# The first feed-forward's input: from rows that are reloaded, scaled and transposed to columns that are stored once, reloaded and scaled

## The chip, the cores and the metric

The kernel runs on one core of one Trainium2 chip. The metric is the device time of one launch in microseconds (us); lower is better. A core has five engines that run side by side, each through its own list of instructions in order: TensorE (PE in the profile; its weight loads are shown as PEld), VectorE (DVE), ScalarE (ACT), GpSimd (POOL) and SyncE (SP), which here issues nearly all DMA transfers. They wait for one another through semaphores.

## The reference

A network of two gated layers over 4 sequences of 1024 tokens, 512 wide. Each layer normalizes its rows, runs an attention and a feed-forward network on the same normalized rows, and multiplies the two:

```python
x = L0_attn_x                                     # (4, 1024, 512)
xn = _layernorm(x, axis=-1)                       # eps 1e-5
s = _L0_attn_ref(xn, Wqkv, bqkv, Wout, bout, slopes)   # linear attention with decay, 16 heads
g = _silu(_L0_ffn_ref(xn, w_fc, w_proj))
x = x + s * g
xn = _layernorm(x, axis=-1)
s = _L1_attn_ref(xn, wq, wk, wv, wo)              # softmax attention, 16 heads
g = _silu(_L1_ffn_ref(xn, wq_gate, ...))
x = x + s * g
return x
```

Layer 0's feed-forward normalizes once more, with another epsilon, inside each of its two linear maps, and uses ternary weights:

```python
def bitlinear(x, w):
    xn = layer_norm(x)                            # eps 1e-6
    x_hat = absmax_quant(xn)                      # in value xn, but for rounding and a clip
    w_hat = ternarize_weights(w)                  # sign(round(w / (mean|w| + eps))) * mean|w|
    return einsum('bsd,od->bso', x_hat, w_hat)
h = gelu(bitlinear(xn, w_fc), approximate=False)  # 512 -> 2048
return bitlinear(h, w_proj)                       # 2048 -> 512
```

So the first feed-forward's input is a layer norm of a layer norm. Since the rows already have mean zero, the second norm is one factor for each token. That factor is what this case is about.

## The kernel before, in words

**Stages.** The 4096 tokens are 8 blocks (`NBLK`) of 512 tokens (`BLK`); a block is 4 tiles (`TPB`) of 128 rows, and the 512 columns are 4 groups of 128 (`KD`). The program runs four stages one after the other: layer 0's attention (up to about 630 us), layer 0's feed-forward (630 to about 1164), layer 1's attention, and layer 1's feed-forward. The change lies in the first two.

**Layer 0's attention.** The loop over `steps` runs over blocks and, in each, over four groups of heads. `moments0` and `norms0` compute four numbers for each token into `st0[blk]`: mean, 1/std, variance, and in column 3 the factor that takes a raw row minus its mean straight to the feed-forward's input. `turn0` normalizes a tile of rows on VectorE, transposes it on TensorE, and ScalarE copies it into `xnTs[blk]`, columns on partitions and tokens along the free axis, 1 MB a block. Beside this, `weights0` loads the feed-forward's weights piece by piece, two pieces a step: VectorE takes sums of their magnitudes and then makes them ternary. At the end, `first_rows` prepares the feed-forward's input for block 0, and the last block's output rows follow (`wo`, L333).

**Layer 0's feed-forward.** The loop over `g` takes one hidden step at a time: block `blk`, and `c`, the group of 128 out of 2048 hidden units. `hidden` multiplies the input by the ternary weights (fc, L588; 8 matmuls into one PSUM buffer of two), ScalarE applies gelu (h, L593), copies the result in a short format (hp, L598) and squares it (L600), VectorE makes the remainder of the split (hp, L601), and GpSimd and VectorE add h and its square to running sums (L609, L610). `proj` multiplies the hidden values into four accumulators, one for each tile of tokens, each two steps behind the one before (pj, L641). Every matmul input is split into two parts, hi and lo, in the short format, `xparts[blk]` for the block's input.

**What lies beside it.** While block `blk` is multiplied, the loop finishes block `blk - 1` and prepares block `blk + 1`. Finishing: `gate` at steps 1, 3, 5 and 7 for one tile of rows each (y on VectorE L658, tanh on ScalarE L660, two products on VectorE L661 and L662, an add on GpSimd L663, the store of the row tile by SP L664), `norm1` at step 12 and `turn_out` (xn on ScalarE L673, transposes tr_x L678). Preparing: at steps 0, 3, 6 and 9 SP loads a tile of the raw rows again (`x0f`, L705); at steps 2, 5, 8 and 11 `prep_in` has VectorE scale it (xq, L568); after the next step `turn_in` transposes it on TensorE (tr_xq, L576) and `split_in` splits it: hi on ScalarE (L230), lo on VectorE (L231), both reading PSUM.

**What sets the order.** TensorE's order is written out by hand, as the program has it. The order of the other engines is set by a planner that places instructions when it expects them to be ready; `keep_in_program_order` pins the ones it is given. Tiles come from pools with a fixed number of buffers (`bufs`), and an instruction waits until the buffer that it writes is free: fc has 2 PSUM buffers, so `fc` of step c+2 needs h of step c to have been read out; h has 3 and the loaded input tiles ("x") have 2.

Of the kernel before, what the change touches and what calls it, by code (L numbers as in the profile page):

```python
# [12 lines left out]
F32 = mybir.dt.float32  # L13
F32R = mybir.dt.float32r
# [5 lines left out]
P = 128  # L20
# [15 lines left out]
def kernel(ctx, tc, ins, out):  # L36
# [59 lines left out]
    nc.vector.memset(one_i, 1)  # L96

    xnT_d = [dram.tile([KD, P, N], F32, tag=f"xnT{b}", name=f"xnT_d{b}") for b in range(B)]

    def moments(pool, src, dst, name, pinned=False):  # L100

# [40 lines left out]
    def transpose_to(dst, src, name, on_scalar):  # L142

        t = tr(f"tr_{name}")
        for k in range(4):
            nc.tensor.transpose(t[:, k, :], src[:, k * P : (k + 1) * P], ident)
        if on_scalar:
            nc.scalar.copy(dst, t)  # L148
        else:
            nc.vector.tensor_copy(dst, t)  # L150
# [73 lines left out]
            w = nxt  # L224
            yield

    def split_in(xp, i, tp):

        hi, lo = [a[:, :, i * P : (i + 1) * P] for a in xp]
        nc.scalar.copy(hi.bitcast(F32R), tp)  # L230
        nc.vector.tensor_tensor(lo.bitcast(F32R), tp, hi, ALU.subtract)  # L231


    with ExitStack() as es:
# [52 lines left out]


        xnTs, vs, oTs = {}, {}, {}
        xparts = {}  # L290

        def moments0(blk):
            st = st0[blk]
            for i in range(TPB):
# [7 lines left out]
        def norms0(blk):  # L302

            st = st0[blk]
            nc.vector.tensor_tensor(st[:, :, 3], st[:, :, 1], st[:, :, 1], ALU.mult)
            nc.vector.tensor_tensor(st[:, :, 3], st[:, :, 3], st[:, :, 2], ALU.mult)
            inv_std(st[:, :, 3], eps6)
            nc.vector.tensor_tensor(st[:, :, 3], st[:, :, 3], st[:, :, 1], ALU.mult)

        def turn0(blk, i):  # L310
            st = st0[blk]
            t = blk * TPB + i
            xn = p2.tile([P, D], F32, tag="xn", name=f"xn0_{t}")
            nc.vector.tensor_scalar(
                xn, xt.pop(t), st[:, i, 0:1], st[:, i, 1:2], ALU.subtract, ALU.mult
            )
            transpose_to(xnTs[blk][:, :, i * P : (i + 1) * P], xn, f"x0_{t}", True)

        def values(blk, i):
            if i == 0:  # L320
# [123 lines left out]
            oTs[blk, g] = p2.tile([P, BLK], F32, tag="oT", name=f"oT0_{nm}", bufs=6)  # L444
            nc.scalar.copy(oTs[blk, g], o)

        def first_rows(i0):

            st = st0[0]
            for i in range(i0, i0 + 2):  # L450
                xq = p2.tile([P, D], F32, tag="xn", name=f"xq_{i}")
                nc.vector.tensor_scalar(
                    xq, xt.pop(i), st[:, i, 0:1], st[:, i, 3:4], ALU.subtract, ALU.mult
                )
                tp = tr(f"tr_xq_{i}")
                for k in range(KD):
                    nc.tensor.transpose(tp[:, k, :], xq[:, k * P : (k + 1) * P], ident)
                split_in(xparts[0], i, tp)

        es.enter_context(tc.manual_schedule(engines={mybir.EngineType.PE}))  # L460

        st = st0[0]
# [37 lines left out]
        for n, (blk, g) in enumerate(steps):  # L500

            if g < 2:
                jobs = [(output, blk - 1, 2 * g + c) for c in range(2)] if blk else []
            else:
                jobs = [(values, blk + 1, 2 * g - 4 + c) for c in range(2)] if blk + 1 < NBLK else []
            if n + 1 == len(steps):
                xparts[0] = xpair("xp_0")
                jobs = [(first_rows, 0), (first_rows, 2)]
            if g == 0 and blk + 1 < NBLK:
                moments0(blk + 1)  # L510
            pts = scores(blk, g, *cur[:2])
            for _ in range(2):
                next(beside, None)
            nxt = None
            if n + 1 < len(steps):
                nxt = project(*steps[n + 1])
            if jobs:
                jobs[0][0](*jobs[0][1:])
            outs(blk, g, cur[2], pts)
            if nxt:  # L520
                kd = turn_k(*steps[n + 1], nxt[1])
            if g < 2 and blk + 1 < NBLK:
                for i in range(2):
# [22 lines left out]
    with ExitStack() as es:  # L546
# [5 lines left out]
        def tr0(name):  # L552
            return pp.tile([P, KD, P], F32, tag="tr", name=name)

        hparts, sums, mvs, x1s, xnTp, x0fs = {}, {}, {}, {}, {}, {}
# [4 lines left out]
        def prep_in(blk, i):  # L560

            st = st0[blk]
            if i == 0:
                xparts[blk] = xpair(f"xp_{blk}")
            t = blk * TPB + i
            x = x0fs.pop(t)
            xq = p2.tile([P, D], F32, tag="xq", name=f"xq_{t}")
            nc.vector.tensor_scalar(  # L568
                xq, x, st[:, i, 0:1], st[:, i, 3:4], ALU.subtract, ALU.mult
            )  # L570
            return lambda: turn_in(blk, i, xq)

        def turn_in(blk, i, xq):
            tp = tr0(f"tr_xq_{blk}_{i}")
            for k in range(KD):
                nc.tensor.transpose(tp[:, k, :], xq[:, k * P : (k + 1) * P], ident)  # L576
            split_in(xparts[blk], i, tp)

        before = None

# [65 lines left out]
        def gate(blk, i):  # L646
# [7 lines left out]
            s = p2.tile([P, D], F32, tag="xq" if last else "s", name=f"s0_{t}")  # L654
            nc.sync.dma_start(out=s, in_=s0_t[t])
            sc = mv[:, 3, i : i + 1]
            y = p2.tile([P, D], F32, tag="y", name=f"y0_{t}")
# [27 lines left out]
                )  # L685

        es.enter_context(tc.manual_schedule(engines={mybir.EngineType.PE}))
        pending = None
        W = {}
        for g in range(NH0 * NBLK + 2 + 2 * TPB):  # L690
            blk, c = divmod(g, NH0)
# [7 lines left out]
                        )  # L699
                    )  # L700
            if blk < NBLK:
                if c % 3 == 0 and c < 3 * TPB and blk + 1 < NBLK:
                    t = (blk + 1) * TPB + c // 3
                    x0fs[t] = p2.tile([P, D], F32, tag="x", name=f"x0f_{t}")
                    nc.sync.dma_start(out=x0fs[t], in_=x_t[t])  # L705
                if c >= 2 and c % 3 == 2 and c < 2 + 3 * TPB and blk + 1 < NBLK:
                    pending = prep_in(blk + 1, (c - 2) // 3)
                hidden(blk, c)
                if blk == 0 and wpj0 + c < NH0:
                    ternary("pj", wpj0 + c, raw0("pj", wpj0 + c, "f"))  # L710
# [14 lines left out]
                gate(blk - 1, c // 2)  # L725
            if blk and c == 12:
                norm1(blk - 1, p2)
            if pending and c % 3 == 0:
                pending()
                pending = None  # L730
# [755 lines left out]
```

## Time and profile before

| | us |
|---|---|
| Median of 3 runs | 3150.0 |
| The three runs | 3148.52, 3150.00, 3150.66 |
| The profiled execution: its time | 3149.29 |
| The profiled execution: span from first to last instruction | 3147.5 |
| TensorE busy in the span | 3088.4 |
| VectorE busy | 1905.1 |
| GpSimd busy | 1501.4 |
| ScalarE busy | 1196.1 |
| Mean granted TensorE clock | 0.994 of full speed |

Most of GpSimd's time is layer 1's attention (844.8 us in one group of additions there), so the sum over the program says little of the stage that is changed. In the time line a row is: start, duration, engine, line, operation, output<-inputs by name, sizes, the number of neighbours taken together, and in brackets the engine's idle time before it and what ended that. Times are microseconds from the span's start.

### The profile page before, as it was taken

Reading aid. Unit: us, or ns where it says so; the run is one execution under the profiler, and the core shown is the slowest. Engines: PE = TensorE matmul, PEld = TensorE weight load, DVE = VectorE, ACT = ScalarE, POOL = GpSimd, SP = SyncE. Lnnn points to the kernel's source line nnn. Section 1 sums busy time; section 2 is a strip of 40 time slices with the busy share of each in tenths; the row PEclk is TensorE's granted clock in tenths of the full one; section 3 lists DMA queues with packets and bytes.
Section 4 is the critical chain, followed back from the end, with each engine's and each line's share of the span. In section 5 each row is a group of like instructions: output and inputs, shape, how many; then the busy total and the mean of one; then the engine's idle time right before and its main releaser. Section 6 shows DMA issues by size and latency. Waiting matters only on the chain.

```text
span 3147.5 us, 61092 instructions
## 1 busy us (share of the span) xinstructions
PE 3088.4 (98%) x26233; PEld 1765.4 (56%) x26233; DVE 1905.1 (61%) x2638; ACT 1196.1 (38%) x1696; POOL 1501.4 (48%) x615
## 2 busy tenths in 40 slices
PE   9999999999999998999999999999999999999998
PEld 5555555578777874443344444334444435888887
DVE  4444555468888775656656555555555684566655
ACT  3111111155555542444444444444444444333332
POOL 0000000034444344898888988888888970000001
PEclk9999999999999999999999999999999999999999
DMA  3111111122222231100001000010000013322211
GB/s 131 54 54 54 54 57 44 38 64 91 81 81 71 94 138 38 48 9 8 8 17 40 12 12 15 20 35 14 10 17 15 12 44 100 119 75 66 67 51 55
DMA packets 97799, 158.46 MB, mean 50 GB/s; under 512 B 13040, under 2 KB 26864, under 8 KB 97392
## 3 DMA queue, kind: packets, MB, share of 16 engines
q1 hardware_dynamic: 96704, 151.33, 15.5%
q8 instruction: 207, 3.39, 0.5%
q0 software_dynamic: 816, 3.15, 0.3%
q14 instruction: 72, 0.59, 0.1%
HBM read 104.10 MB, written 41.94 MB: 46 GB/s over the span
## 4 chain that ended last, share of the span: by engine, by line
PE 84%; DVE 11%; issue 2%; ACT 2%; POOL 1%; SPq 1%; DMA 0%; ACTq 0%; POOLq 0%; DVEq 0%
PE sk L1027 9%; PE sq L1000 8%; PE y L1046 8%; PE qk L350 7%; PE gate L1218 5%; PE up L1218 5%; PE dn L1240 5%; PE v1ps L856 4%; PE v0ps L324 3%; PE wo L333 3%; PE wo L856 3%; PE wq L856 3%; PE fc L588 3%; PE wk L856 3%; PE pj L641 3%; PE sk L1033 2%
## 5 line engine op out<-in xcount | busy, mean ns | idle before, releaser
L1067 POOL TENSOR_TENSOR part<-part,pT 128x2048 f32<-128x2048 f32 x184 | 844.8, 4591 | 25.7 <-ACT pT L1038 16.5
L1004 DVE TENSOR_REDUCE mx<-sq 128x2 f32<-128x1024 f32 x512 | 603.3, 1218 | 384.3 <-PE sq L1000 383.1
L1038 ACT ACTIVATE pT<-sk 128x1024 f32<-128x1024 f32 x512 | 496.3, 1021 | 619.4 <-PE sk L1033 616.1
L1027 PE MATMUL sk<-wqT,wkT 32*128 32x512 f32 x2048 | 332.5, 645 | 4.3 <-DVE mx L1004 4.3
L1000 PE MATMUL sq<-wkT,wqT 32*128 32x512 f32 x2048 | 322.5, 641 | 6.1 <-ACT pT L1038 5.1
L1046 PE MATMUL y<-pT,v 128*32 128x512 f32 x2048 | 276.3, 610 | 0.2 <-ACT pT L1038 0.2
L609 POOL TENSOR_TENSOR sums<-sums,h 128x512 f32<-128x512 f32 x112 | 162.9, 1455 | 228.9 <-ACT h L593 223.8
L641 PE MATMUL pj<-wpj,hp 128*128 128x512 f32 x1024 | 265.2, 397 | 5.8 <-DVE hp L601 4.9
L588 PE MATMUL fc<-xp,wfc 128*128 128x512 f32 x1024 | 261.1, 397 | 2.9 <-ACT h L593 2.0
L1262 POOL TENSOR_TENSOR th<-th,x 128x512 f32<-128x512 f32 x31 | 40.1, 1295 | 457.9 <-DVE th L1261 377.0
L1033 PE MATMUL sk<-mT,onesr 2*128 2x512 f32 x1024 | 239.3, 788 | 2.2 <-DVE mT L1016 2.2
L357 POOL TENSOR_TENSOR qd<-qT,wqkv 128x512 f32<-128x512 f32 x32 | 41.1, 1285 | 405.0 <-ACT qT L355 379.1
L350 PE MATMUL qk<-xnT,wqkv 128*128 128x512 f32 x512 | 230.0, 602 | 0.7 <-ACT xnT L148 0.7
L641 PEld LDWEIGHTS pj<-wpj,hp 128*128 128x128 f32 x1024 | 190.0, 188 | 58.2 <-DVE hp L601 17.4
L588 PEld LDWEIGHTS fc<-xp,wfc 128*128 128x128 f32 x1024 | 187.3, 188 | 44.4 <-ACT h L593 5.0
L1027 PEld LDWEIGHTS sk<-wqT,wkT 32*128 32x128 f32 x2048 | 99.9, 184 | 138.0 <-issue 111.4
L1218 PE MATMUL gate<-xp,wf 128*128 128x512 f32 x704 | 174.1, 389 | 0.0
L1065 POOL TENSOR_TENSOR part<-pT,pT 128x2048 f32<-128x2048 f32 x31 | 141.2, 4555 | 69.0 <-ACT pT L1038 68.8
L1218 PE MATMUL up<-xp,wf 128*128 128x512 f32 x704 | 173.8, 389 | 0.0
L1240 PE MATMUL dn<-wf,hp 128*128 128x512 f32 x704 | 173.5, 389 | 0.0
L601 DVE TENSOR_TENSOR hp<-h,hp 128x512 fp32r<-128x512 f32 x128 | 116.9, 913 | 76.2 <-ACT hp L598 76.1
L350 PEld LDWEIGHTS qk<-xnT,wqkv 128*128 128x128 f32 x512 | 95.2, 191 | 112.8 <-issue 104.2
(219 smaller groups left out, 4543.4 us busy)
## 6 DMA issues: line engine op xcount, KB each, us to landing
s<-s SPq DMA_DIRECT2D x96, 256.0 KB
x<-x SPq DMA_DIRECT2D x36, 256.0 KB
x<-in_x SPq DMA_DIRECT2D x32, 256.0 KB
raw_fc<-in_w_fcT SPq DMA_DIRECT2D x32, 256.0 KB
x0f<-in_x SPq DMA_DIRECT2D x32, 256.0 KB
x0r<-in_x SPq DMA_DIRECT2D x32, 256.0 KB
x<-th SPq DMA_DIRECT2D x32, 256.0 KB
xnT<-xnT_d SPq DMA_DIRECT2D x8, 1024.0 KB
```

The lines of the kernel that those rows point to most:

```text
L350: nc.tensor.matmul(a, lhsT=wqkv[k][:, c0 : c0 + P], rhs=xnTs[blk][:, k, :], start=(k == 0), stop=(k == KD - 1),)
L588: nc.tensor.matmul(a, lhsT=wfc[k][:, c * P : (c + 1) * P], rhs=xp[n][:, k, :].bitcast(F32R), start=(k == 0 and n == 0), stop=(k == KD - 1 ...
L641: nc.tensor.matmul(ds[i], lhsT=hparts[blk, c][n][:, i * P : (i + 1) * P], rhs=wpj[c], start=(c == 0 and n == 0), stop=(c == NH0 - 1 and n ...
L856: nc.tensor.matmul(out[r0 : r0 + HD, :], lhsT=lhsT[:, r0 : r0 + HD], rhs=rhs, start=start, stop=stop,)
L1000: nc.tensor.matmul(sq[:, hh, :], lhsT=qT[r, q0 : q0 + P], rhs=kT[r, n * 512 : (n + 1) * 512], start=True, stop=True,)
L1004: nc.vector.tensor_reduce(mx[:, qt, 2 * pair : 2 * pair + 2, n], sq, AX.X, ALU.max)
L1027: nc.tensor.matmul(sks[h // 2][:, h % 2, :], lhsT=kT[r, kb * P : (kb + 1) * P], rhs=qT[r, qh * 512 : (qh + 1) * 512], start=True, stop=False,)
L1038: nc.scalar.activation(pT[:, 2 * pair : 2 * pair + 2, :], sks[pair], AF.Exp, scale=QKS)
L1046: nc.tensor.matmul(y[r, :], lhsT=v[:, kb, r], rhs=pT[:, h, :], start=(kb == 0), stop=(kb == TB - 1),)
L1067: add.tensor_tensor(parts[u], parts[u], pT, ALU.add)
L1218: nc.tensor.matmul(a, lhsT=ws[n, c][:, k, :], rhs=xp[m][:, k, :], start=(k == 0 and m == 0), stop=(k == KD - 1 and m == 1),)
L1240: nc.tensor.matmul(ds[i], lhsT=hparts[blk, c][n][:, i * P : (i + 1) * P], rhs=w, start=(c == 0 and n == 0), stop=(c == NH1 - 1 and n == 1),)
```

## The change

The normalized, transposed rows that the attention has anyway (`xnTs[blk]`) are stored to DRAM, 1 MB a block, as soon as a block's four tiles are turned. `norms0` leaves out its last multiply, so that column 3 of the statistics is the factor from the normalized row to the feed-forward's input, and this is stored to DRAM too, as a row of 512 numbers. The feed-forward then loads column groups of the transposed rows (256 KB each) where it loaded row tiles, and once a block the row of factors, broadcast to all 128 partitions (256 KB). GpSimd multiplies a column group by the factors, ScalarE makes hi, and GpSimd makes lo. The loads are issued at steps 0, 3, 6 and 9 and the split at steps 2, 5, 8 and 11, as before. `prep_in`, `turn_in`, `split_in` and `first_rows` go. Block 0's input is loaded two steps before the end of the attention and split in its last step, where `output` of the last attention block follows directly. The row load of `x0r` in `gate` stays.

```diff
+    xn0T_d = [
+        dram.tile([KD, P, BLK], F32, tag=f"xn0T{i}", name=f"xn0T_d{i}") for i in range(NBLK)
+    ]
+    more_d = dram.tile([NBLK, BLK], F32, tag="more", name="more_d")
...
-    def split_in(xp, i, tp):
-
-        hi, lo = [a[:, :, i * P : (i + 1) * P] for a in xp]
-        nc.scalar.copy(hi.bitcast(F32R), tp)
-        nc.vector.tensor_tensor(lo.bitcast(F32R), tp, hi, ALU.subtract)
+    def ffn_in(blk, k, tile):
+
+        if k == 0:
+            xparts[blk] = xpair(f"xp_{blk}")
+            mores[blk] = tile("more", f"more_{blk}")
+            nc.sync.dma_start(out=mores[blk], in_=more_d[blk].partition_broadcast(P))
+        x = tile("x", f"x0f_{blk}_{k}")
+        tc.keep_in_program_order(nc.sync.dma_start(out=x, in_=xn0T_d[blk][k]))
+
+        def split():
+            hi, lo = [a[:, k, :] for a in xparts[blk]]
+            nc.gpsimd.tensor_tensor(x, x, mores[blk], ALU.mult)
+            nc.scalar.copy(hi.bitcast(F32R), x)
+            nc.gpsimd.tensor_tensor(lo.bitcast(F32R), x, hi, ALU.subtract)
+
+        return split
...
             inv_std(st[:, :, 3], eps6)
-            nc.vector.tensor_tensor(st[:, :, 3], st[:, :, 3], st[:, :, 1], ALU.mult)
+            nc.sync.dma_start(out=more_d[blk].rearrange("(i p) -> p i", p=P), in_=st[:, :, 3])
...
             transpose_to(xnTs[blk][:, :, i * P : (i + 1) * P], xn, f"x0_{t}", True)
+            if i == TPB - 1:
+                nc.sync.dma_start(out=xn0T_d[blk].rearrange("k p n -> p k n"), in_=xnTs[blk])
...
-        def first_rows(i0):
-
-            st = st0[0]
-            for i in range(i0, i0 + 2):
-                xq = p2.tile([P, D], F32, tag="xn", name=f"xq_{i}")
-                nc.vector.tensor_scalar(
-                    xq, xt.pop(i), st[:, i, 0:1], st[:, i, 3:4], ALU.subtract, ALU.mult
-                )
-                tp = tr(f"tr_xq_{i}")
-                for k in range(KD):
-                    nc.tensor.transpose(tp[:, k, :], xq[:, k * P : (k + 1) * P], ident)
-                split_in(xparts[0], i, tp)
...
-            if n + 1 == len(steps):
-                xparts[0] = xpair("xp_0")
-                jobs = [(first_rows, 0), (first_rows, 2)]
...
             if n + 2 == len(steps):
 
-                for i in range(TPB):
-                    xt[i] = p2.tile([P, D], F32, tag="x", name=f"x0f_{i}", bufs=4)
-                    tc.keep_in_program_order(nc.sync.dma_start(out=xt[i], in_=x_t[i]))
+                first_in = [
+                    ffn_in(
+                        0, k,
+                        lambda tag, name: p2.tile(
+                            [P, BLK], F32, tag={"more": "xn"}.get(tag, tag), name=name,
+                            bufs={"x": 4}.get(tag, 2),
+                        ),
+                    )
+                    for k in range(KD)
+                ]
+            if n + 1 == len(steps):
+                for split in first_in:
+                    split()
...
             if blk < NBLK:
-                if c % 3 == 0 and c < 3 * TPB and blk + 1 < NBLK:
-                    t = (blk + 1) * TPB + c // 3
-                    x0fs[t] = p2.tile([P, D], F32, tag="x", name=f"x0f_{t}")
-                    nc.sync.dma_start(out=x0fs[t], in_=x_t[t])
-                if c >= 2 and c % 3 == 2 and c < 2 + 3 * TPB and blk + 1 < NBLK:
-                    pending = prep_in(blk + 1, (c - 2) // 3)
+                if blk + 1 < NBLK:
+                    if c % 3 == 2 and c < 3 * KD:
+                        split()
+                    if c % 3 == 0 and c < 3 * KD:
+                        split = ffn_in(
+                            blk + 1, c // 3,
+                            lambda tag, name: p2.tile([P, BLK], F32, tag=tag, name=name),
+                        )
                 hidden(blk, c)
...
-            if pending and c % 3 == 0:
-                pending()
-                pending = None
```

More of the change, by code (lines that the diff above doesn't have):

```diff
@@ L225, in weights0 @@
             yield
-    def split_in(xp, i, tp):
-        hi, lo = [a[:, :, i * P : (i + 1) * P] for a in xp]
-        nc.scalar.copy(hi.bitcast(F32R), tp)
-        nc.vector.tensor_tensor(lo.bitcast(F32R), tp, hi, ALU.subtract)
+    def ffn_in(blk, k, tile):
[11 more added lines that the diff above has]
+        return split
+    xparts, mores = {}, {}
     with ExitStack() as es:
@@ L289 @@
         xnTs, vs, oTs = {}, {}, {}
-        xparts = {}
         def moments0(blk):
@@ L553, in tr0 @@
             return pp.tile([P, KD, P], F32, tag="tr", name=name)
-        hparts, sums, mvs, x1s, xnTp, x0fs = {}, {}, {}, {}, {}, {}
+        hparts, sums, mvs, x1s, xnTp = {}, {}, {}, {}, {}
         for c in range(wpj0, NH0):
@@ L558 @@
         rows = p2.tile([P, D], F32, tag="rows", name="rows", bufs=1)
[L560 to L577, printed above, removed]
         before = None
@@ L653, in gate @@
             nc.sync.dma_start(out=x, in_=x_t[t])
-            s = p2.tile([P, D], F32, tag="xq" if last else "s", name=f"s0_{t}")
+            s = p2.tile([P, D], F32, tag="more" if last else "s", name=f"s0_{t}")
             nc.sync.dma_start(out=s, in_=s0_t[t])
@@ L727 @@
                 norm1(blk - 1, p2)
-            if pending and c % 3 == 0:
-                pending()
-                pending = None
             if 0 < blk < NBLK and c >= 14:
```

## The prediction

> **What bounds the kernel now.** I read the page's busy times first, then two stretches of the stage that the change touches (one steady block, 831 to 898 us), then the time line in it.
>
> ```profile
> PE 3088.4 (98%) x26233; PEld 1765.4 (56%) x26233; DVE 1905.1 (61%) x2638; ACT 1196.1 (38%) x1696; POOL 1501.4 (48%) x615
> ```
> ```profile
> 831.00:866.00 35.00, 34.42 (x158) 27.39 (x158) 31.07 (x54) 17.45 (x30) 15.03 (x10) 1.00 0.36 113
> 866.00:898.00 32.00, 31.62 (x153) 25.64 (x152) 23.97 (x39) 20.94 (x35) 13.49 (x9) 1.00 0.15 43
> ```
> The columns of the second fence are stretch, length, then busy PE, PEld, DVE, ACT, POOL. TensorE is 98% busy here too, so work taken off it looks like pure gain. But in the first half of a block, where gating runs, VectorE is 31.07 of 35.00 busy. The time line shows why that matters:
>
> ```profile
> 854.97 1.81 DVE L662 SCALAR_TENSOR_TENSOR th<-th,mv,s 128x512 f32<-128x512 f32 x1
> 856.70 0.68 DVE L601 TENSOR_TENSOR hp<-h,hp 128x512 fp32r<-128x512 f32 x1
> 856.86 1.67 POOL L663 TENSOR_TENSOR th<-th,x0r 128x512 f32<-128x512 f32 x1 [0.63 <-DVE th L662]
> 857.31 1.77 DVE L610 TENSOR_TENSOR sums<-sums,sq 128x512 f32<-128x512 f32 x1
> 859.61 0.67 DVE L231 TENSOR_TENSOR xp<-tr_xq,xp 128x512 fp32r<-128x512 f32 x1
> ...
> 861.92 0.74 DVE L658 SCALAR_TENSOR_TENSOR y<-rows,mv,pj 128x512 f32<-128x512 f32 x1
> 862.69 0.72 ACT L660 ACTIVATE th<-y,mv 128x512 f32<-128x512 f32 x1 [4.47 <-DVE y L658]
> 863.32 0.67 ACT L593 ACTIVATE h<-fc,gam_fc 128x512 f32<-128x512 f32 x1
> 864.04 2.11 PE L588 MATMUL fc<-xp,wfc 128*128 128x512 f32 x8 [0.26 <-ACT h L593]
> ```
> Two things. First, a VectorE operation with two SBUF inputs takes 0.68 alone and 1.77 to 1.81 while GpSimd works; the subtract of the input split (L231), which has one input in PSUM, takes 0.67 in the same stretch. Second, the last four lines are a chain: y on VectorE, its tanh on ScalarE, the gelu h queued behind that, and fc_10, which needs the PSUM buffer h gives back. TensorE waits only 0.26, but without slack: whatever makes y later moves fc_10.
>
> **The change part by part.** *TensorE.* Each block loses 4 groups of transposes:
>
> ```profile
> 809.51 0.60 PE L576 MATMUL tr_xq<-ident,xq 128*128 128x128 f32 x4
> 809.86 2.09 PE L588 MATMUL fc<-xp,wfc 128*128 128x512 f32 x8
> 811.78 2.00 PE L641 MATMUL pj<-wpj,hp 128*128 128x512 f32 x8
> 813.63 1.99 PE L588 MATMUL fc<-xp,wfc 128*128 128x512 f32 x8
> 815.45 2.02 PE L641 MATMUL pj<-wpj,hp 128*128 128x512 f32 x8
> 817.31 0.60 PE L678 MATMUL tr_x<-ident,xn 128*128 128x128 f32 x4
> ```
> The step with a group is 809.51 to 813.63 = 4.12, the next 813.63 to 817.31 = 3.68: a group is worth 0.44 in the pipeline (not its 0.60). 32 groups make 14.1 us, the most that TensorE can gain directly.
>
> *The other engines, per block.* VectorE loses 4 xq (0.73 mean) and 4 subtracts (0.67). ScalarE's 4 casts stay, now from SBUF (0.62 like L598's, not 0.57). GpSimd gets 8 operations of 128x512: a multiply by the token scale and a subtract for each of 4 column tiles, with the cast between them. Nearest rows: L357's multiply 1.285 alone, L609's add 1.455 as a mean of alone and contended. 8 × 1.3 = 10.4 more on an engine 28.5 of 67 busy: room as an engine. The cost is VectorE's.
>
> Here the row is that th (L662) and sums (L610) go from 0.7 to 1.8 beside GpSimd. The Trainium skill, "SBUF — State Buffer", section "Who interferes with whom", says that a VectorE operation with two SBUF inputs and a GpSimd operation exclude each other for the length of the instruction, whoever is first, and that one with at most one SBUF input is free. It speaks against this change: the removed subtract (PSUM input) took no part, all eight new operations do. By the rule, each holds the other for its full lone time (1.30 and 0.68). The trace's alternating pairs are shorter: three GpSimd adds from 867.69 take 5.16 with a VectorE operation between them, so one pair is about 1.71, of which I give 1.16 to GpSimd and 0.55 to VectorE (VectorE's contended operations end about 0.55 after GpSimd's). I take the trace's holds and keep the rule's for the range. Demand for the shared port per block by lone times: before, 19 GpSimd × 1.3 + 39 VectorE × 0.6 + 1.8 for xq = 50 of 66.6 us (829.69 to 896.31, from one block's sums to the next's on TensorE); after, 27 × 1.3 + 23.4 = 59 of the 64.8 that four groups less would leave.
>
> I then walked one block with the new order of each engine (numbers behind a name are steps or tiles; the multiply, cast and subtract of column tile k are mult_k, hi_k, lo_k): GpSimd runs sums_6, the add of row tile 10, sums_7, mult_2, lo_2, sums_8; ScalarE runs hi_2, then the tanh of tile 11, then h_8. GpSimd holds 1.16, VectorE 0.55. On before's time axis:
> - fc_8 starts about 854.5, as h_6 ends 854.45; nothing is gained over 854.89 but 0.4, though TensorE would be ready at 853.99.
> - GpSimd: sums_6 to 855.6, then, between VectorE's th, hp_6 and sums_6, tile 10's add 856.7 to 857.9, sums_7 to 859.6. The row tile's store goes out at 857.95; the load of column tile 2 stands behind it on SP's queue, 858.3, and is there 2.8 later (first load of the program: 0.75 issue to 3.52 use; x0f 630.78 to 633.65), 861.1. So mult_2 waits for it: it ends 862.3, cast hi_2 862.9. Tanh of tile 11 is queued behind that cast on ScalarE: 863.55; h_8 864.2; fc_10 starts 864.25 against 864.04 before, while TensorE was ready about 862.
> - lo_2, sums_8 and tile 11's add share the port; tile 3's load is issued 868.5, lands 871.3; mult_3 ends 872.5, hi_3 873.1, h_10 (behind it) 873.75, so fc_12 starts 873.8 against 872.02: 1.8 late. At step 12 the missing transposes give some back: 877.5 against 876.47.
> - VectorE, in turn, is held 1.16 by each of GpSimd's further operations and is behind when gating ends: sums_12 ends 882.8, the norm's small operations (2.6) 885.4, xn 886.2. The transposes tr_x of the finished rows, which stand in TensorE's order, start 886.2 against 883.92.
>
> So a steady block is 2.3 longer (1.4 if the loads land in 2.2; 4.0 with the rule's full holds). Sum:
> - blocks 2 to 6, which run beside the next block's preparation: 5 × 2.3 = 11.5
> - block 1 the same plus 1.7, because cast hi_1 is also in front of hp_5 on ScalarE: 4.0
> - block 0, where VectorE also quantizes the last weights and 16 GpSimd operations meet 25 of VectorE in eight steps (hp_2 about 646 against 640.69, partly absorbed): 5, between 3 and 8
> - end of the attention stage: the transpose groups at 609.28 and 614.79 and a wait of 0.68 at the second go, so the first output product starts about 614.1 and not 615.71: −1.6
>
> Total +18.9. The profiled execution took 3149.3 (span 3147.5 and 1.8 around it): 3168. The median of the runs is 0.7 above it, which I leave out.
>
> *Costed at nothing, with the cover.* Eight 1 MB stores and the 256 KB broadcast loads: DMA share is 0.16 to 0.17 from 100 to 595 us, and 0.36 at most in the block above. The first store meets the weight loads at 2 to 26 us (share 0.93); it can push the decay table by about 3 us, to 25, so dec is ready about 33.5; the first product needs it at 40.3. The scale's store waits on SP for VectorE's reciprocal and holds back the ternary weights' loads behind it (107.6 to 109.6), whose reductions stand on VectorE: their buffer is needed at 114.8 and they would end about 112.9; uncovered it is up to 1 us in each of 7 blocks. Its four-byte elements are 512 a block; no row prices them, nobody waits before the next stage. Zero to 7 in all for these; I take zero, since the margin exceeds 0.6 everywhere that I followed it. ScalarE's casts, 0.05 longer: ScalarE is idle 17 of 35.
>
> **The rivals.**
> - *Heavier lock (20%).* The full lone durations hold. 5 × 4.0 + 5.7 + 8 − 1.6 = +32: 3181. For: the rule, and L610 at 1.77. Against: the shorter pairs at 867.69.
> - *Gain just eaten (17%).* Loads or GpSimd are a little earlier than I walk, tanh and h come as before, and TensorE starts the same steps at the same time with a wait in place of the transposes: about 3148. For: that chain holds to within 0.3 in before already. Against: nothing takes the 1.8 of fc_12 away.
> - *The other side: GpSimd's work hides (18%).* All 14.1 comes, with 1.9 of waits for xq and 0.7 at the stage's start: 16.7, so 3133. The place is h_8: it must end before TensorE is ready for fc_10, about 862, so mult_2 must be done by about 860.3. My walk has 862.3. It would take a load that doesn't wait for the store of the tile before, or ScalarE running tanh ahead of the cast. For: VectorE has 5.6 less to do per block; GpSimd is under half busy.
> - *The change does nothing of what it says*: the transposes are named by line and gone, so I give this no share.
>
> **How the numbers follow.** My own case: 45%, 3156 to 3176, at 3168. 0.2% is 6.3 us, about what a measurement of this kernel tells from no change. Faster (under 3143): 0.18, GpSimd's work hidden. Same: 0.17. Slower: 0.45 + 0.20 = 0.65. The range goes from 3141 (into the gap between no change and the gain, with the fast case out) to 3190 (heavy lock plus the uncovered stores); it leaves out 0.18 below and little above.
>
> **What would show it.** In after: tr_xq gone; GpSimd busy up by 80 to 100 us, its multiplies idle before with a DMA (x0f) as releaser; hp (L601) and sums (L610) means up from 913 and 1082 ns; fc idle behind h of ScalarE up from 2.0 us to over 15, or tr_x waiting for xn; a steady block 69 instead of 66.6. I am wrong if fc's waits stay under 5 us and hp's mean doesn't rise (then the gain comes), or if the attention stage grows by more than 2 us (then the stores were not covered).

## The result and the profile after

The changed kernel took 3258.31 us (median of 5 runs, 3251.15 to 3267.73) against 3150.66 (5 runs, 3148.52 to 3153.63): 1.0343 times the time of before, interval 1.0331 to 1.0356. It is slower, as forecast, but by 108 us and not by 19, and far outside the range.

Where do the 108 us lie? The table takes from both time lines the start of the first fc, of each group that sums a block's statistics (ms), and of layer 1's first product (wk):

| stretch | before | after | difference | forecast |
|---|---|---|---|---|
| start to first fc (attention stage) | 630.49 | 711.47 | +80.98 | −1.6 |
| first fc to block 0's sums | 67.31 | 69.89 | +2.58 | +5 |
| block 1 | 65.31 | 68.87 | +3.56 | +4.0 |
| blocks 2 to 6, each (mean) | 66.57 | 70.73 | +4.17, five times 20.84 | +2.3, five times 11.5 |
| last block and the end of the stage | 68.16 | 68.14 | −0.02 | 0 |

Three quarters of the loss are in a stage where a small gain was expected. The engines' totals of after show little of it, only that TensorE's share fell from 98% to 95%:

```profile
PE 3102.6 (95%) x26105; PEld 1766.3 (54%) x26105; DVE 1886.8 (58%) x2566; ACT 1194.5 (37%) x1696; POOL 1595.9 (49%) x679
```

GpSimd has 94 us more, as forecast. TensorE has 128 instructions fewer and is busy 14 us longer, so its instructions themselves became slower. The time line of after from 125 us on shows where the stage's time goes (rows as before; SPq and the line number mark a DMA issue by SP):

```profile
125.11 0.38 SPq L324 DMA_DIRECT2D more_d<-st  x1
125.54 0.97 SPq L183 DMA_DIRECT2D raw_fc<-in_w_fcT  x2
...
138.60 0.69 DVE L188 TENSOR_REDUCE part_fc<-raw_fc 128x1 f32<-128x512 f32 x1 [13.51 <-DMA raw_fc<-in_w_fcT]
...
139.80 0.68 DVE L387 TENSOR_TENSOR kd<-k0t,kdec 128x512 f32<-128x512 f32 x1
...
140.53 1.11 PE L151 MATMUL tr_x<-ident,xn 128*128 128x128 f32 x4 [10.47 <-DVE kd L387]
...
141.44 5.02 PE L351 MATMUL wo<-wout,oT 128*128 128x512 f32 x8
```

The same place in before:

```profile
114.31 0.66 PE L146 MATMUL tr_x<-ident,xn 128*128 128x128 f32 x4 [0.35 <-DVE kd L369]
114.80 3.60 PE L333 MATMUL wo<-wout,oT 128*128 128x512 f32 x8
```

The token factors go out at 125.11. The weight load issued 0.43 later is there only 13 us after its issue. VectorE's reduction stands waiting for it with kd behind it, and TensorE waits 10.47 for kd. VectorE's waits of this stage say that it happened seven times (columns: total, times, longest):

```profile
DVE part_fc L188 <- DMA raw_fc<-in_w_fcT: 23.9, 2, 13.5
DVE part_pj L188 <- DMA raw_pj<-in_w_projT: 22.8, 2, 11.5
DVE neg_fc L213 <- DMA raw_fc<-in_w_fcT: 22.5, 2, 13.8
...
DVE neg_pj L213 <- DMA raw_pj<-in_w_projT: 13.0, 1, 13.0
```

Together 82.2 us. The stretches from 126 to 144 show the second part of the price (the column before the last two is the granted clock, as a share of full speed):

```profile
126.00:128.00 2.00, 2.00 (x15) 1.29 (x16) 0.00 (x0) 0.00 (x0) 0.78 (x1) 1.00 0.64 145
...
134.00:136.00 2.00, 0.00 (x0) 0.00 (x0) 0.00 (x0) 0.00 (x0) 0.00 (x0) 0.51 0.19 5
...
142.00:144.00 2.00, 2.00 (x3) 0.68 (x2) 0.24 (x1) 0.27 (x1) 0.00 (x0) 0.50 0.69 182
```

After about 4 us without work the clock is halved and stays so for a while after work returns: the eight wo matmuls at 141.44 take 5.02 instead of 3.60. Over the stage the groups of after, and then wo of before, read

```profile
L351 PE MATMUL wo<-wout,oT 128*128 128x512 f32 x256 | 124.1, 633 | 0.0
...
L151 PE MATMUL tr_x<-ident,xn 128*128 128x128 f32 x128 | 22.9, 307 | 61.0 <-DVE kd L387 59.0 <-DVE st L479 1.2 <-DVE xn L330 0.5
...
L333 PE MATMUL wo<-wout,oT 128*128 128x512 f32 x256 | 114.6, 592 | 0.0
```

The transposes tr_x took 20.0 before, with 4.9 of waiting for kd. TensorE's waits in this stage grew by 64.6 us (tr_x for kd 54.1, qk 6.9, u 3.6); most of the other 16 us is the half clock, 9.5 of it in wo alone.

The second place is the one that the prediction walked. This is after's step 8 to 10 of a steady block, 91.45 us later than in before:

```profile
950.55 0.42 SPq L239 DMA_DIRECT2D x0f<-xn0T_d  x1
...
953.36 1.29 POOL L243 TENSOR_TENSOR x0f<-x0f,more 128x512 f32<-128x512 f32 x1 [1.51 <-DMA x0f<-xn0T_d]
954.68 0.62 ACT L244 CAST xp<-x0f 128x512 fp32r<-128x512 f32 x1 [5.32 <-POOL x0f L243]
955.20 0.72 ACT L653 ACTIVATE th<-y,mv 128x512 f32<-128x512 f32 x1
...
955.83 0.67 ACT L586 ACTIVATE h<-fc,gam_fc 128x512 f32<-128x512 f32 x1
...
956.55 3.68 PE L581 MATMUL fc<-xp,wfc 128*128 128x512 f32 x8 [1.93 <-ACT h L586]
```

Load, multiply, cast, tanh, h, fc_10: the forecast's chain link by link. The y of that tile was there at 953.66, so the tanh stood behind the cast. TensorE's wait for h before fc_10 grew from 0.26 to 1.93.

The eight matmuls of this fc_10 take 3.68 instead of 2.11, because the clock is halved here too:

```profile
957.00:959.00 2.00, 2.00 (x6) 1.55 (x5) 1.96 (x3) 1.97 (x5) 1.37 (x2) 0.50 0.00 0
```

It happens three times in after's feed-forward, for about 3.5 us each, and not in before's. It does not explain the longer blocks: those that have it in blocks 2 to 6 took 70.36 and 70.37, the others 70.80 to 71.23.

### The profile page after: what moved, and what is told of

Same layout as the page of the kernel before. It is cut to its first block, busy times and chain, and to the rows that moved or that the text cites. A ratio compares the mean times of both kernels' runs of the same rounds, so it can differ in the third digit from the quotient of the medians.

```text
span 3256.5 us, 60856 instructions
## 1 busy us (share of the span) xinstructions
PE 3102.6 (95%) x26105; PEld 1766.3 (54%) x26105; DVE 1886.8 (58%) x2566; ACT 1194.5 (37%) x1696; POOL 1595.9 (49%) x679
## 4 chain that ended last, share of the span: by engine, by line
PE 76%; DVE 9%; DMA 5%; ACT 4%; issue 3%; POOL 3%; SPq 1%; POOLq 0%; ACTq 0%; DVEq 0%
PE sk L1018 9%; PE sq L991 8%; PE y L1037 8%; PE qk L368 5%; PE gate L1209 5%; PE up L1209 5%; PE dn L1231 5%; PE v1ps L847 3%; PE wo L847 3%; PE wq L847 3%; PE wk L847 3%; PE wo L351 3%; PE v0ps L342 3%; PE fc L581 2%; PE sk L1024 2%
## 5 line engine op out<-in xcount | busy, mean ns | idle before, releaser
L581 PE MATMUL fc<-xp,wfc 128*128 128x512 f32 x1024 | 262.8, 400 | 25.0 <-ACT h L586 24.3
L602 POOL TENSOR_TENSOR sums<-sums,h 128x512 f32<-128x512 f32 x112 | 171.0, 1527 | 137.8 <-ACT h L586 136.5
L581 PEld LDWEIGHTS fc<-xp,wfc 128*128 128x128 f32 x1024 | 189.8, 189 | 73.2 <-ACT h L586 32.5
L594 DVE TENSOR_TENSOR hp<-h,hp 128x512 fp32r<-128x512 f32 x128 | 132.1, 1032 | 95.7 <-ACT hp L591 95.7
```

Source lines behind the costliest of these rows:

```text
L581: nc.tensor.matmul(a, lhsT=wfc[k][:, c * P : (c + 1) * P], rhs=xp[n][:, k, :].bitcast(F32R), start=(k == 0 and n == 0), stop=(k == KD - 1 ...
```

## The experiments

In the table, "blocks" is the mean of blocks 2 to 6. r1 to r4 and r7 to r11 are one profiled execution each; before took 3152 to 3155 (median) beside the various runs.

| run | first fc | blocks | total |
|---|---|---|---|
| before / after | 630.5 / 711.5 | 66.57 / 70.73 | 3150.7 / 3258.3 |
| r1_rows: factors stored as rows | 628.8 | 70.90 | 3170.6 |
| r2_elem_only: before, with the element store | 703.7 | 66.51 | 3218.3 |
| r8_elem_actq: after, store on ScalarE's queue | 637.9 | 70.80 | 3183.9 |
| r3_rows_dve: r1, split on VectorE | 628.7 | 67.18 | 3151.3 |
| r4_rows_nomult: r1 without the multiply | 630.0 | 67.57 | 3154.1 |
| r7_rows_early: r1, loads earlier | 630.4 | 68.60 | 3160.9 |
| r11_before_pool8: before, with idle GpSimd work | 628.8 | 71.18 | 3177.1 |
| r9_rows_dve_late: r3, split later | 628.6 | 67.37 | 3155.0 |
| s2_scaled_late: scaled in the attention stage | 632.1 | 66.62 | 3149.5 |
| s3_scaled_later: s2, split later still | 631.5 | 67.42 | 3151.6 |
| r10_rows_none: no preparation | 628.7 | 63.98 | 3133.6 |
| v1_presplit: split in the attention stage | 631.9 | 64.00 | 3129.6 |

**r1_rows: is it the form of the store?** My theory for the 81 us: the store takes 512 separate elements of four bytes, and what is issued behind it in the queue lands late.

```diff
-            nc.sync.dma_start(out=more_d[blk].rearrange("(i p) -> p i", p=P), in_=st[:, :, 3])
+
+        def more_row(blk):
+            tp = tr(f"more_{blk}")[:TPB, 0, :]
+            nc.tensor.transpose(tp, st0[blk][:, :, 3], ident)
+            row = p2.tile([P, D], F32, tag="xn", name=f"row_{blk}")[:TPB, :P]
+            nc.scalar.copy(row, tp)
+            nc.sync.dma_start(out=more_d[blk].rearrange("(i p) -> i p", p=P), in_=row)
...
         norms0(0)
+        more_row(0)
...
                     turn0(blk + 1, 2 * g + i)
+                if g == 0:
+                    more_row(blk + 1)
```

> The changed kernel, but the 512 factors are turned into four rows of 128 by a small transpose on TensorE and stored as four rows of 512 bytes instead of 512 elements of four bytes. Theory 'element store' (the store of single elements holds the DMA queue for about 11 us, so the weight load issued behind it lands late and VectorE stands in its reduction, 7 times): the feed-forward starts at 631 to 635 instead of 711, the total is about 3178 (3174 to 3186), and a block of the feed-forward still takes about 70.7. Rival 'the 1 MB stores and SP's waits' (the bulk of the new traffic, or the store's wait in SP's order): the start stays after 690 and the total over 3230.

The first fc started at 628.80: 1.69 earlier than before, where the prediction had 1.6 for this stage. Start and total (3170.62) lie a little below the expected bands, and blocks stayed at 70.9. The same 2 KB as four rows cost nothing that shows. The 1 MB stores and the broadcast loads, which remain, are covered.

The edit also moves the store: loads of rows now stand behind it, and the weight loads come only 3.9 us after it. Would a store of elements have been harmless there? That was not run. But the store of rows is itself done quickly: xn, which needs its buffer back, runs 1.27 us after the issue.

```profile
114.55 0.27 SPq L330 DMA_DIRECT2D more_d<-row  x1
...
115.82 0.55 DVE L336 TENSOR_SCALAR xn<-x,st 128x512 f32<-128x512 f32 x1 [1.48 <-DMA more_d<-row]
```

**r2_elem_only: is the store enough?**

```diff
             nc.vector.tensor_tensor(st[:, :, 3], st[:, :, 3], st[:, :, 1], ALU.mult)
+            nc.sync.dma_start(out=more_d[blk].rearrange("(i p) -> p i", p=P), in_=st[:, :, 3])
```

> The kernel before with one addition: the element store of 512 four-byte values per block (of the old factor, which nobody reads), at the same place. Theory 'element store': the feed-forward starts at 700 to 715 with 7 waits of 10 to 14 us on weight loads, blocks stay at 66.6, total 3220 to 3235. Rival 'the 1 MB stores and SP's waits': the start moves by under 10 us, total under 3162.

The store alone (and the DRAM tensor that it writes) makes the kernel of before 3218.32 us, just below the expected band, with the first fc at 703.66 and blocks at 66.5. That is 73.2 us of the 82.7 that separate after from r1; what the other new traffic adds to the stalls was not taken apart. VectorE's waits are the same kind, if shorter:

```profile
DVE part_pj L185 <- DMA raw_pj<-in_w_projT: 21.7, 2, 11.0
DVE neg_fc L210 <- DMA raw_fc<-in_w_fcT: 20.0, 2, 10.9
DVE part_fc L185 <- DMA raw_fc<-in_w_fcT: 18.0, 3, 9.5
```

**r8_elem_actq: the queue, or all DMA?**

```diff
-            nc.sync.dma_start(out=more_d[blk].rearrange("(i p) -> p i", p=P), in_=st[:, :, 3])
+            nc.scalar.dma_start(out=more_d[blk].rearrange("(i p) -> p i", p=P), in_=st[:, :, 3])
```

> The changed kernel with the element store issued by ScalarE on its own queue instead of SP's; nothing else. If the loads were late because they stand behind the store in the same queue: the feed-forward starts at 630 to 645, total 3170 to 3190. Rival: the 512 four-byte writes occupy what all queues share, so the weight loads are late all the same: start over 690, total over 3235.

With the same 512 elements on ScalarE's own queue the first fc comes at 637.92, and the waits for weight loads after 90 us are down to these:

```profile
DVE part_pj L188 <- DMA raw_pj<-in_w_projT: 0.4, 1, 0.4
DVE neg_fc L213 <- DMA raw_fc<-in_w_fcT: 0.2, 1, 0.2
```

So the repeated delay belongs to the queue: what stands behind the store in it waits. The 7.4 us that are left over before are one wait, at the very first store. There SP stands 6.6 us before it issues the load of a bias, put down to this store, so the decay table's load goes out at 22.16 instead of 16.10 in r1, and TensorE waits 7.36 for what needs it:

```profile
SPq L293 <- DMA more_d<-st: 6.6, 1, 6.6
```

Here the other queue helped wherever nothing waited for the store itself. The Trainium skill ("DMA: Bandwidth & Descriptors", section "Queues, rings and completion order") says that each DMA engine takes turns between the queues it has work for and takes the descriptors of one queue in order, and this pair of runs agrees: 711.5 and 637.9. It gives no time for such a store; that is measured here.

**r3, r4, r7, r11: the 27 us in the feed-forward.** Two mechanisms were in the prediction: GpSimd and VectorE exclude each other, and the column load stands behind the store of a row tile and in front of a cast, a tanh and an h. r3 moves the multiply and the subtract, r4 leaves the multiply out, r7 issues the loads earlier, r11 adds GpSimd work to before whose results nobody reads.

```diff
 r3
-            nc.gpsimd.tensor_tensor(x, x, mores[blk], ALU.mult)
+            nc.vector.tensor_tensor(x, x, mores[blk], ALU.mult)
             nc.scalar.copy(hi.bitcast(F32R), x)
-            nc.gpsimd.tensor_tensor(lo.bitcast(F32R), x, hi, ALU.subtract)
+            nc.vector.tensor_tensor(lo.bitcast(F32R), x, hi, ALU.subtract)
 r4
-            nc.gpsimd.tensor_tensor(x, x, mores[blk], ALU.mult)
 r7
-                    if c % 3 == 0 and c < 3 * KD:
+                    if c in (0, 1, 3, 6):
 r11
             nc.vector.tensor_scalar(
                 xq, x, st[:, i, 0:1], st[:, i, 3:4], ALU.subtract, ALU.mult
             )
+            for _ in range(2):
+                nc.gpsimd.tensor_tensor(x, x, x, ALU.mult)
```

> r1 with the multiply and the subtract of the input split on VectorE instead of GpSimd. Theory 'lock' (GpSimd's eight operations a block exclude VectorE's two-input operations): a block falls from about 70.7 to 66 to 67.5, waits of fc for h fall from 24 us to under 10, total 3145 to 3162. Rival 'late loads' (the column tiles are loaded behind the store of the row tile on SP's queue and the cast stands in front of the gelu on ScalarE): a block stays at 69.5 or more, total over 3168.

> r1 without the multiply by the token factor (that part of the computation is left out; the factor row is still stored and loaded): GpSimd has four operations a block fewer, the loads and the cast stand where they were. Theory 'lock': half of the added GpSimd work goes, a block takes 67.5 to 69, total 3155 to 3168. Rival 'late loads': the cast now waits for the load itself, a block stays at 70 or more, total over 3172.

> r1 with the column loads issued earlier (steps 0, 1, 3 and 6 instead of 0, 3, 6 and 9; each still two buffers), everything else in its place: GpSimd's multiply no longer waits for a load that stands behind the store of a row tile. Theory 'lock': the waits of the multiply for the load (26 us in the changed kernel) vanish, but a block stays at 70 to 71 (total 3165 to 3175), because the same operations exclude VectorE. Rival 'late loads', which is the prediction's own chain (load lands, multiply, cast, tanh behind the cast): a block falls to 68 or less, total under 3156.

> The kernel before with eight more GpSimd operations of 128x512 per block (squares, in place, of the loaded rows after VectorE has used them; no engine needs the results), at the places where the rows are scaled. It measures the exclusion alone, with no load, cast or chain behind it. Theory 'lock': hp's mean rises from 913 by 50 ns or more and a block from 66.6 to 68 to 69.5, total 3158 to 3172. Rival: work of GpSimd that nobody waits for costs nothing, a block under 67, total under 3155.

r3 came to 67.18 a block and r4 to 67.57, as the lock theory had it (r4's total, 3154.14, is just below its band). Both also shorten the chain in front of the cast, so they do not show the lock alone. r7 came to 68.60, between the two theories: the multiply's waits for its load fell only from 28.2 us in r1 (25.9 in after) to 15.7, and that already gave back 2.3 of the 4.3 us a block (block 0 lost 3.0 by it). So the late load is a real half of a steady block's loss, and it and the lock are not separate sums: what is late in the chain is late because GpSimd, VectorE and ScalarE all stand in it. r11 leaves load, cast and reader out, and the effect is stronger than expected (71.18 against 68 to 69.5): eight operations add 4.6 us to a block, 0.58 for each. VectorE's groups, first hp in before, then r11:

```profile
L601 DVE TENSOR_TENSOR hp<-h,hp 128x512 fp32r<-128x512 f32 x128 | 116.9, 913 | 76.2 <-ACT hp L598 76.1
...
L603 DVE TENSOR_TENSOR hp<-h,hp 128x512 fp32r<-128x512 f32 x126 | 136.7, 1085 | 66.4 <-ACT hp L600 66.4
...
L105 DVE BATCH_NORM_STATS2 bs_c<-th 128x6 f32<-128x512 f32 x28 | 19.1, 684 | 7.1 <-POOL th L665 7.1
...
L231 DVE TENSOR_TENSOR xp<-tr_xq,xp 128x512 fp32r<-128x512 f32 x28 | 18.8, 671 | 0.0
```

hp, with two inputs in SBUF, rises from 913 to 1085 ns; the subtract with its input in PSUM stays at 671 (670 before). The exclusion is thus seen, but r11 is not the exclusion alone: the added work also stands in front of GpSimd's own operations. VectorE waits 7.1 us for GpSimd's add of a finished row tile (1.2 before). How much of the 4.6 us each takes was not separated.

**r9, s2, s3: where the 14.1 us of transposes went.** r3 has no added GpSimd work and no transposes, and still no gain on before. r9 moves its splits to steps 8, 10, 12 and 14. s2 also scales the block in place on GpSimd in the attention stage, after its last use there, and keeps only the cast and VectorE's subtract in the feed-forward. s3 moves these to steps 11, 12, 14 and 15 (and block 0's subtracts to GpSimd).

```diff
 s2
+        def scale0(blk):
+            for k in range(KD):
+                x = xnTs[blk][:, k, :]
+                nc.gpsimd.tensor_tensor(x, x, mores[blk], ALU.mult)
+            nc.sync.dma_start(out=xn0T_d[blk].rearrange("k p n -> p k n"), in_=xnTs[blk])
...
             hi, lo = [a[:, k, :] for a in xparts[blk]]
-            nc.gpsimd.tensor_tensor(x, x, mores[blk], ALU.mult)
             nc.scalar.copy(hi.bitcast(F32R), x)
-            nc.gpsimd.tensor_tensor(lo.bitcast(F32R), x, hi, ALU.subtract)
+            nc.vector.tensor_tensor(lo.bitcast(F32R), x, hi, ALU.subtract)
```

> r3_rows_dve with the loads at steps 4, 6, 9 and 11 and the splits at 8, 10, 12 and 14, so that little of the split falls into the first half of a block, where gating keeps VectorE busy. Theory: TensorE's gain of 1.76 a block was eaten in r3 by the chain y, tanh, h of the first half; out of that half the period falls from 67.1 to 64.5 to 66, total 3130 to 3142. Rival: the second half has its own limit (norm1 behind VectorE, then xn, tr_x), or the added two-input operations cost as much anywhere: a block at 66.5 to 68, total 3147 to 3158.

> The multiply by the factor moved into the attention stage: GpSimd scales the transposed rows in place after their last use there and the scaled block is stored; the factor is stored as rows and loaded back as in r1. In the feed-forward only the cast on ScalarE and the subtract on VectorE are left, at steps 8, 10, 12 and 14. GpSimd is idle over 90% of the attention stage and has few two-input VectorE operations against it there, so the attention stage should end as in r1 (first fc 627 to 633). Theory lock and chain: with four operations a block on VectorE and none on GpSimd, a block takes 64.8 to 65.8, total 3128 to 3140, a gain of 0.3 to 0.7% on before. Rival: the first half's chain doesn't depend on the split at all and a block stays at 66.4 to 67: total 3145 to 3152.

> s2_scaled_late with the splits later still, at steps 11, 12, 14 and 15 (loads at 7, 9, 12 and 13), because in s2 two of the four subtracts still ran inside the gating half; and with block 0's subtracts on GpSimd, because in s2 the last attention step took 15.6 instead of 12.7 us. Theory chain: the first half keeps its period of before, and the second half, where VectorE has room, takes the splits: a block falls to 65 to 66, first fc at 629 to 630, total 3135 to 3145. Rival: the block is bound by gating and VectorE's tail wherever the split stands: 66.3 to 67, total 3146 to 3152, no difference from before.

All three fell to their rivals: 67.37, 66.62 and 67.42 a block (s3's is even above its rival's band). s2's ratio to before is 0.9989 (0.9978 to 1.0000), s3's 0.9993 (0.9985 to 1.0001): neither is clear of no change. So moving the split within the block does not bring the gain. TensorE's waits in s3's feed-forward say what took the gain:

```profile
PE fc L599 <- ACT h L604: 13.3, 13, 2.1
PE tr_x L689 <- ACT xn L684: 7.5, 6, 1.4
PE pj L652 <- DVE hp L612: 3.8, 10, 1.0
```

24.6 us, where before had 8.8 (pj for hp 4.9, fc for h 2.0, tr_xq for xq 1.9). At each place tried, a cast on ScalarE and a two-input subtract on VectorE give TensorE new waits about as large as the transposes that they replace (15.8 us more here, against 14.1).

**r10_rows_none: the floor.** This run leaves the preparation out, so that every block is multiplied with block 0's input, to see what is there to win.

```diff
-                    if c % 3 == 2 and c < 3 * KD:
-                        split()
-                    if c % 3 == 0 and c < 3 * KD:
+                    if c == 0:
+                        xparts[blk + 1] = xparts[blk]
+                    if False:
                         split = ffn_in(
```

> r1 without any preparation of the input in the feed-forward: every block is multiplied with block 0's input (the loads, multiplies, casts and subtracts of blocks 1 to 7 are left out). It is the floor for any way of preparing the input elsewhere. Theory chain (part of the 1.76 us a block that the transposes cost is hidden, because gating's chain sets the first half): a block takes 65.4 to 66.3, total 3136 to 3144. Rival, TensorE is the bound once the rest is gone: a block takes 64.3 to 64.9, total 3126 to 3133.

63.98 a block, below both bands, and the stage takes 514.4 us instead of 533.6. So 19 us were to be had, more than the 14.1 of the transposes; the versions that left work for the input on VectorE, ScalarE or GpSimd there got nothing measurable of it.

**v1_presplit: nothing but loads.** The attention stage multiplies as in s2, makes both parts and stores them.

```diff
...
+            for k in range(KD):
+                x = xnTs[blk][:, k, :]
+                hi = p2.tile([P, BLK], F32, tag="s", name=f"hi_{blk}_{k}")
+                nc.scalar.copy(hi.bitcast(F32R), x)
+                nc.gpsimd.tensor_tensor(x.bitcast(F32R), x, hi, ALU.subtract)
+                nc.sync.dma_start(out=xn0T_d[blk][0][k], in_=hi)
+            nc.sync.dma_start(out=xn0T_d[blk][1].rearrange("k p n -> p k n"), in_=xnTs[blk])
...
+    def ffn_in(blk):
+        xparts[blk] = xpair(f"xp_{blk}")
+        for n in range(2):
+            tc.keep_in_program_order(
+                nc.sync.dma_start(
+                    out=xparts[blk][n], in_=xn0T_d[blk][n].rearrange("k p n -> p k n")
+                )
+            )
```

> The whole preparation moved into the attention stage: GpSimd multiplies the transposed rows by the factor (stored as rows and loaded back), ScalarE casts hi, GpSimd subtracts lo in place, both parts are stored (2 MB a block) and loaded straight into the matmul's input tiles, one 1 MB load each. No engine but SP does anything for the input in the feed-forward. Theory: a block reaches r10's floor of 64.0 instead of 66.6, the feed-forward takes 514 to 517 instead of 533.6, and the attention stage ends as before within 4 us, since GpSimd has room there and few two-input VectorE operations stand against it: total 3131 to 3140, 0.4 to 0.6% faster than before. Rival: in the attention stage the stores of hi and lo, which wait for ScalarE and GpSimd, stand in front of the weight loads on SP's queue, and what the feed-forward gains is lost there: first fc after 640, total 3142 or more.

3129.58 us (6 runs, 3126.17 to 3140.06), 0.9932 times before (0.9916 to 0.9947): it beats both kernels, and lies just below the expected band. The stretches of the attention stage and the feed-forward, and two consecutive sums of TensorE's time line, 63.98 apart:

```profile
0.00:630.00 630.00, 616.55 (x3854) 346.18 (x3855) 306.91 (x613) 116.92 (x213) 129.44 (x118) 1.00 0.28 93
630.00:1144.00 514.00, 506.44 (x2297) 409.53 (x2296) 384.81 (x641) 286.54 (x469) 220.89 (x151) 1.00 0.30 101
```
```profile
886.30 1.84 PE L623 MATMUL ms<-ones,sums 128*128 128x1 f32 x16
...
950.28 1.84 PE L623 MATMUL ms<-ones,sums 128*128 128x1 f32 x16
```

In the attention stage GpSimd is now busy 129 of 630 us instead of 46, ScalarE 117 instead of 100, and the stage ends 1.4 us later than in before, 3.1 later than in r1. The operations that cost the feed-forward 27 us cost the attention stage about 3.

## Why the prediction was wrong

- **The step that failed: "Its four-byte elements are 512 a block; no row prices them, nobody waits before the next stage."** I looked for a reader of the stored data and found none near. The one who waits is not a reader: it is the next load in the same queue, and behind it VectorE, and behind that TensorE. I had followed exactly that load for SP's own delay (2 us) and put the bound at 7 us in all, without a price for the transfer itself. Measured: 81 us for the stage, shown by storing rows instead (r1), by adding the element store alone (r2, 73 us) and by moving it to another queue (r8). The decay table, which the walk had there at 25, is used from 24.83 in r1 but only from 32.37 in after. An operation that no row prices should have had a wide upper end, not zero.
- **The attention stage without it came out as forecast, in part by luck**: −1.69 in r1 against −1.6. The missing transposes at its end give 1.15 (from the last u to the first output product 7.44 instead of 8.59). The other 0.54 was there before: the first projection took 7.13 instead of 8.83, and r1's eight small transposes took some of that back.
- **The feed-forward's mechanism was right, its size too small.** Its signs came out: fc waits 24.3 us for h, the multiplies 25.9 for their load, and the means of hp and sums rose to 1032 and 1175 ns. 27.0 us against 20.5 for blocks 0 to 6. Block 1 came out at +3.6 (4.0), block 0 at +2.6 (5). The mis-sized term is the steady block, +4.17 instead of +2.3. On before's axis the walk had the load issued at 858.3 (measured 859.1), the multiply's end at 862.3 (863.2), fc_10 at 864.25 (865.1), fc_12 at 873.8 (875.1) and tr_x at 886.2 (887.6). Each link took about what I gave it (2.8 from load to multiply: 2.81), but the error grows from 0.5 at fc_8 to 1.4 at tr_x. What makes it grow was not taken apart.
- **The choice between rule and row went the wrong way for a steady block.** Holding the port for the full lone time gave 4.0, the shorter pairs of the trace 2.3. The measured 4.17 is nearer to the longer holds, though no run separates the length of a hold from the rest of the chain, and for blocks 0 to 6 together the full holds gave 33.7 where 27.0 came. The Trainium skill ("SBUF — State Buffer", section "Who interferes with whom") gives the hold for the whole instruction where it speaks of VectorE's two-port modes; that it holds for two SBUF inputs as well was my reading. The demand on the port was also summed too low: with VectorE's own lone time of 0.68, and not 0.6, it is 62 of 64.8 us, not 59.
- **"Gain just eaten"** did not come true for this change: r1 is still 17 us slower than before. It describes r3, s2 and s3, which lose the transposes and gain nothing measurable.
- **"GpSimd's work hides"** is refuted by r1, which has the element store out of the way and still blocks of 70.9. The 16.7 us that it promised are there, and more, in the version that keeps GpSimd, VectorE and ScalarE out of it (v1).

## What to carry to other kernels

A transfer can cost by its number of elements and not by its bytes (2 KB here), and those who wait for it include what is issued behind it in its queue; so look at what stands behind a store in its queue, not only at who reads it. When TensorE looks like the bound at 98%, taking work from it paid here only when the replacement did not land on the engines that return its buffers; the work moved to a stage where those engines are idle cost about 3 us there and brought 19.

## What the runs showed of the hardware

- A 2 KB store of single four-byte elements delayed the loads behind it in the same queue by about 10 us (13 from issue to use, against 2.8 for the load at 950.55); from another queue it delayed only what waited for it (r8). In after 544 small packets lie between 126 and 127 us, and most packets of the loads behind the store come at 137 to 139. In between, 2 to 9 packets of 2 KB or so pass in a microsecond. At 130 to 131, shown second, three of them fill 43.4% of the DMA engines' time, so the queue is not still but very slow. What makes it so was not tried.

```profile
DMA packets 640, 0.21 MB, mean 213 GB/s; under 512 B 544, under 2 KB 544, under 8 KB 639
...
DMA packets 3, 0.01 MB, mean 6 GB/s; under 512 B 0, under 2 KB 0, under 8 KB 3
...
q1 hardware_dynamic: 3, 0.01, 43.4%
```

- A stall of 10 us costs more than itself: the granted clock is 0.50 from about 4 us into the stall until at least 3 us after it; over all the stalls of the stage this is most of the 16 us that the waits do not explain. The Trainium skill ("TensorE: Matmul & The Clock Gate", section "Part 1: The HAM clock gate") states that the clock is halved after an idle window of about 3.4 us; the rows at 134 and 142 us agree. The feed-forward of after does not: there the clock fell to 0.50 after waits of only 1.78 to 1.93 us (fc at 815.32, 956.55 and 1026.89), while a wait of 2.12 (885.85) left it at 1.00. What sets it there stays open.
- GpSimd work that nobody needs is not free: in r11 each 128x512 operation made a block 0.58 us longer. VectorE's two-input operations took longer beside it, and GpSimd's own adds came later; the share of each is open.
